# Two layers of graph attention on one core: where the second pass of layer 0 makes its masks, and in what order it issues its loads

## The chip, the cores and the metric

The kernel runs on one core of one Trainium2 chip, in float32. The metric is device time in microseconds (us). A tile has 128 partitions. TensorE is called PE in profiles (PEld is its weight load), VectorE DVE, ScalarE ACT, GpSimd POOL and SyncE SP.

## The reference

There are 4096 nodes with 512 features. Only layer 0 matters for the change. In it:

```
h = relu(layernorm(x))
node_att = softmax(h @ node_w, axis=0)
e = (h @ edge_w) @ (h @ edge_w).T            # 4096 x 4096, symmetric
e = where(adj > 0, e, -9e15)
edge_att = softmax(e, axis=1)
x = x + (adj * node_att * edge_att) @ (h @ weight) + bias
```

Layer 1 normalizes again and runs an attention with 8 heads over the same adjacency. Its logits are sums of a source and a target term.

## The kernel before, in words

The program has four stages, one after the other.

The first normalizes x and computes `sup` = h @ weight, kept in SBUF, and h @ edge_w, transposed. The second, the first pass over the scores, computes the upper half of the symmetric matrix e on TensorE (L288), stores it in device memory as `e_d`, and finds each row's maximum under the mask.

The third stage is the second pass of layer 0 (L321 to L594), and the change is there. It goes through 8 blocks b of 512 columns and, inside each, 32 tiles m of 128 rows, 256 steps in all. A tile is the transposed piece of the attention: 128 source nodes by 512 target nodes. For each:

- `load` (L337) issues on SP the load of `a`, the tile of adj transposed (256 KB, L356, 11 buffers). For tiles above the diagonal (m // 4 < b) it also loads the scores `et` as they are stored (L353); this text calls them direct tiles. For the four tiles on the diagonal it loads pieces of rows into `eb` (L349). At m = 0 it issues on GpSimd's queue the load of the row maxima `mb` (L342).
- `squares` (L359) serves tiles below the diagonal, whose scores are only stored as their mirror image. Once per four tiles it issues on SP 16 DMAs of 64 KB each (L366) into one `eb` tile (four buffers), which permute blocks of 32 x 32 so that VectorE's transpose of 32 x 32 blocks can finish the work.
- `turn` (L370) makes the transposed scores in PSUM: VectorE's transpose (L378) for squares, TensorE transposes (L384) for pieces on the diagonal, nothing for direct tiles.
- `exps` (L390) makes the mask `mk` = -9e15 where adj is 0 (L392, a tensor_scalar on VectorE), subtracts the maxima (L396), adds the mask to give `d` (L397), all on VectorE, and issues exp on ScalarE (L399).
- `weigh` (L402) multiplies by adj on VectorE, which gives `at` (L405, three buffers), and adds exp to the running sum `racc` on GpSimd (L412 once per block, L415 after).
- `gather` (L418) multiplies `at` with `sup` on TensorE: 4 products, 8 matmul instructions in the profile, into four PSUM banks (L435). At m = 8 it issues four loads of 256 KB on SP (L425). At the last tile of a block the row sums (L432) come before the products, and ScalarE copies the result out (L440).

After `weigh`, `finish` (L445) scales one of the four row tiles of the block before, on VectorE (L454), and stores it from GpSimd's queue (L455), in steps 2 to 5 of a block; `tail` (L529) feeds the start of the next part. In steps 3 and 4 of the first block `maxima` of the last column block is done as well.

The order of instructions in each engine's queue is that in which these functions are called: the loop at L564 to L576, with a list of stages and how many tiles each is ahead. The order of one step on VectorE is therefore: transpose of tile s+3, mask, subtraction and addition of tile s+2, product of tile s+1, and then what `finish` adds. On SP it is: squares (at every fourth step) for tiles s+11 to s+14, then scores and `a` of tile s+8. Queues run in order; an instruction that waits for a buffer or for data holds those behind it on its engine.

The fourth stage is layer 1 (from L596 on). The end of the third stage already computes its linear part (L505).

Of the kernel before, what the change touches and what calls it, by code (L numbers as in the profile page):

```python
# [8 lines left out]
FP = mybir.dt.float32  # L9
AF = mybir.ActivationFunctionType  # L10
ALU = mybir.AluOpType
# [4 lines left out]
P = 128  # L16
NEG_BIG = -9000000000000000.0
# [11 lines left out]
def kernel(  # L29
# [15 lines left out]
    nc = tc.nc  # L45
# [6 lines left out]
    BL = 512  # L52
# [47 lines left out]
    with tc.tile_pool(name="w0", bufs=1) as wp, tc.tile_pool(name="a0", bufs=2) as ap_, tc.tile_pool(  # L100
        name="a0s", bufs=8
# [126 lines left out]
    def maxima(i, acc, psum, pool):  # L228

        mx = pool.tile([P, TB], FP, name="mx")  # L230
        nc.vector.tensor_reduce(mx, rm[:, i * TB:(i + 1) * TB, i:NB], AX.X, ALU.max)
        pc = psum.tile([P, TB, P], FP, name="pt")
        for j in range(TB):
            nc.tensor.transpose(pc[:, j, :], acc[:, j * P:(j + 1) * P], ident)
        cm = pool.tile([P, TB], FP, name="cm")
        nc.vector.tensor_reduce(cm, pc, AX.X, ALU.max)
        nc.vector.tensor_tensor(mx, mx, cm, ALU.max)
        yield
        pm = psum.tile([P, BL], FP, name="pt")
        nc.tensor.transpose(pm[:TB, 0:P], mx, ident)  # L240
        ms = pool.tile([TB, P], FP, name="ms")
        nc.vector.tensor_copy(ms, pm[:TB, 0:P])
        nc.gpsimd.dma_start(mx_d[i], ms)


    with tc.tile_pool(name="mx", bufs=1) as mxp, tc.tile_pool(name="b_a", bufs=6) as adjp, tc.tile_pool(
        name="b_e", bufs=4
    ) as esp, tc.tile_pool(name="b_m", bufs=2) as mkp, tc.tile_pool(name="b_s", bufs=2) as sp, tc.tile_pool(
        name="b_p", bufs=6, space=PSUM
# [3 lines left out]
        loaded, masks = {}, {}  # L253
# [67 lines left out]
    with tc.tile_pool(name="c_a", bufs=11) as adjp, tc.tile_pool(name="c_b", bufs=4) as ebp, tc.tile_pool(  # L321
        name="c_e", bufs=9
    ) as etp, tc.tile_pool(name="c_w", bufs=3) as wkp, tc.tile_pool(name="c_t", bufs=3) as atp, tc.tile_pool(
        name="c_m", bufs=2
    ) as mxp, tc.tile_pool(name="c_o", bufs=4) as iop, tc.tile_pool(name="c_s", bufs=2) as sp, tc.tile_pool(
        name="c_p", bufs=1, space=PSUM
    ) as p_o, tc.tile_pool(name="c_q", bufs=3, space=PSUM) as p_t, tc.tile_pool(
        name="c_r", bufs=1, space=PSUM
    ) as p_r, tc.manual_schedule():
        steps = [(b, m) for b in range(NB) for m in range(NT)]  # L330
        blk = {}
        src, pts, aj, ex, at = {}, {}, {}, {}, {}

        def rows_of(m):
            return slice(m * P, (m + 1) * P)
# [34 lines left out]
        def turn(b, m):  # L370
# [16 lines left out]
                parts.append((slice(n * P, BL), eb[:, i, :] if m // TB == b else eb))  # L387
            src[b, m] = parts

        def exps(b, m):  # L390
            mk = wkp.tile([P, BL], FP, name="mk")
            nc.vector.tensor_scalar(mk, aj[b, m], 0.0, NEG_BIG, ALU.is_le, ALU.mult)  # L392
            d = wkp.tile([P, BL], FP, name="d")
            pt = pts.pop((b, m))
            for cs, part in src.pop((b, m)):
                nc.vector.tensor_tensor(pt[:, cs], part[:, cs], blk[b][0][:, cs], ALU.subtract)  # L396
            nc.vector.tensor_tensor(d, pt, mk, ALU.add)  # L397
            e = wkp.tile([P, BL], FP, name="ex")
            nc.scalar.activation(e, d, AF.Exp)  # L399
            ex[b, m] = e  # L400
# [44 lines left out]
        def finish():  # L445

            t, acc, oc, rs, xt = left.pop(0)
            b, j = divmod(t, TB)
            if j == 0:
                sc = sp.tile([P, TB], FP, name="sc")  # L450
                nc.vector.reciprocal(sc, rs)
                nc.vector.tensor_tensor(sc, sc, na[:, b * TB:(b + 1) * TB], ALU.mult)
                scale[b] = sc
            nc.vector.scalar_tensor_tensor(oc, acc, scale[b][:, j:j + 1], xt, op0=ALU.mult, op1=ALU.add)  # L454
            nc.gpsimd.dma_start(x1[rows_of(t), :], oc)  # L455
# [71 lines left out]
        end = len(steps)  # L527

        def tail(s):  # L529

            if s == -6:
                w_fetch()
            if -6 <= s and s + 6 < NT:
                fetch(s + 6)
            if s == -2:
                stats(0)
                stats(1)
                norm(0)
                stats(2)
                norm(1)  # L540
            if s >= 0:
                if 0 < s:
                    values(s - 1)
                if s + 2 < NT:
                    norm(s + 2)
                if s + 3 < NT:
                    stats(s + 3)
                if s == 0:
                    turn_h(0)
                if s + 1 < NT:  # L550
                    turn_h(s + 1)
                linear(s)
                if s > 1:
                    logits(s - 2)
                if s == WT + 2:

                    pt = p_t.tile([P, BL], FP, name="pt")
                    for h in range(HG):
                        nc.tensor.transpose(pt[:WT, h * P:(h + 1) * P], s_n[:, h, 0:WT], ident)
                    st = sp.tile([WT, HG, P], FP, name="s_t", bufs=1)  # L560
                    nc.vector.tensor_copy(st.rearrange("t h p -> t (h p)"), pt[:WT, :])
                    nc.gpsimd.dma_start(s_d.rearrange("h t p -> t h p"), st)

        stages = ((squares, 11), (load, 8), (turn, 3), (exps, 2), (weigh, 1), (gather, 0))  # L564
        for s in range(-11, end):
            for f, ahead in stages:
                if 0 <= s + ahead < end:
                    f(*steps[s + ahead])
                if f is weigh:
                    if left and s % NT > 1:  # L570
                        finish()
                    tail(s - end)
                    if s == 3:
                        ending = maxima(NB - 1, acc_z, p_t, sp)
                    if s in (3, 4):
                        next(ending, None)  # L576
# [10 lines left out]
        pt = p_t.tile([P, BL], FP, name="pt")  # L587
# [50 lines left out]
    with tc.tile_pool(name="p", bufs=2) as prp, tc.tile_pool(name="rl", bufs=2) as rlp, tc.tile_pool(  # L638
        name="io1", bufs=3
    ) as iop, tc.tile_pool(name="s1", bufs=1) as sp, tc.tile_pool(name="za", bufs=1) as zp0, tc.tile_pool(name="e3", bufs=2) as e3p, tc.tile_pool(  # L640
        name="zb", bufs=1
    ) as zp1, tc.tile_pool(name="e", bufs=3) as ep, tc.tile_pool(name="ac", bufs=2) as acp, tc.tile_pool(
        name="os", bufs=1
    ) as osp, tc.tile_pool(name="u", bufs=1) as usp, tc.tile_pool(
        name="p_x", bufs=1, space=PSUM
    ) as p_x, tc.tile_pool(name="p_v", bufs=1, space=PSUM) as p_v, tc.tile_pool(
        name="p_t1", bufs=1, space=PSUM
# [4 lines left out]
        zs_, ra, ex, e3, rl, pr, acc, pv, late = {}, {}, {}, {}, {}, {}, {}, {}, {}  # L652
# [272 lines left out]
        load(0, 2)  # L925
        first_e = ra[0, 0]
        exps(0, 0)
        ra[0, 0] = first_e

# [28 lines left out]
        scale(0, 1)  # L958

        stages = ((load, 3), (logs, 5), (exps, 1), (weigh, 1), (factors, 2), (scale, 2), (gather, 0))  # L960
        for s in range(len(steps)):
            for f, ahead in stages:
# [45 lines left out]
```

## Time and profile before

| | us |
|---|---|
| median of 3 runs | 2991.66 (2991.22 to 2992.32) |
| the profiled execution: time | 2991.82 |
| the profiled execution: span, first to last instruction | 2990.0 |
| busy in the span: TensorE | 2942.8 (98%) |
| busy in the span: VectorE | 2607.1 (87%) |
| busy in the span: GpSimd | 1340.9 (45%) |
| second pass of layer 0: first product on TensorE | starts at 716.53 |
| second pass of layer 0: row sums of block 7 | start at 1622.10 |
| VectorE's masks of this pass (L392), 256 | 219.3 in all, 0.857 each |
| VectorE's products (L405), 256 | 193.5 in all, 0.756 each |
| GpSimd's running sums (L415), 240 | 323.5 in all, 1.348 each |
| SP's loads of squares (L366), median to landing | 2.9 |

A row of groups reads: line, engine, operation, output<-inputs, shape, number; then busy time in all, the mean in ns; then the engine's idle time ahead of these instructions, and what ended it. A row of the timeline reads: start, duration, engine, line, operation, names, number. A row of the table by stretches reads: the stretch, its length, the busy time of each engine with its number of instructions, the granted clock of TensorE (1.00 is full), the share of the DMA engines and GB/s.

### The profile page before, as it was taken

The numbers are of one execution on the slowest core, as the hardware profiler recorded it, in microseconds if no ns is written. First come the engines' busy times: TensorE is split into PE (matmuls) and PEld (weight loads), VectorE is DVE, ScalarE is ACT, GpSimd is POOL, SyncE is SP. The second block draws the span as 40 slices with busy tenths as digits, with TensorE's granted clock in tenths as the row PEclk, the third lists the DMA queues.
The fourth block names the chain that finished last, engine by engine and source line by source line (L and its number), as shares of the span: only waits on it lengthen the run. The fifth ranks groups of instructions, "written<-read, shape, count | busy, mean of one in ns | idle before, by whom it ended". The sixth has DMA issues, their size and how long they took to land.

```text
span 2990.0 us, 43039 instructions
## 1 busy us (share of the span) xinstructions
PE 2942.8 (98%) x15371; PEld 1155.0 (39%) x15371; DVE 2607.1 (87%) x3596; ACT 1325.5 (44%) x1852; POOL 1340.9 (45%) x1042
## 2 busy tenths in 40 slices
PE   8999999998999999999999989999999999999998
PEld 4444444444344444444444433323222322232222
DVE  5434777778999999998997789999999999999998
ACT  2111111111112122122122368888777777777776
POOL 3401111112333343443443657575757575757574
PEclk9999999999999999999999999999999999999999
DMA  4205666667875674664553239696969696979795
GB/s 155 95 7 185 224 219 223 227 217 181 195 169 153 156 184 149 173 190 144 177 179 110 62 113 226 199 247 198 249 201 242 204 243 208 237 209 237 213 228 156
DMA packets 454055, 552.01 MB, mean 185 GB/s; under 512 B 261624, under 2 KB 287256, under 8 KB 453840
## 3 DMA queue, kind: packets, MB, share of 16 engines
q1 hardware_dynamic: 400816, 387.81, 42.1%
q0 software_dynamic: 51008, 157.51, 22.8%
q10 hardware_dynamic: 2016, 3.93, 0.4%
q8 instruction: 121, 1.98, 0.3%
q14 instruction: 94, 0.77, 0.1%
HBM read 409.47 MB, written 59.97 MB: 157 GB/s over the span
## 4 chain that ended last, share of the span: by engine, by line
PE 76%; DVE 11%; DMA 4%; SPq 3%; issue 3%; ACT 2%; POOL 0%; DVEq 0%; ACTq 0%; POOLq 0%
PE pv L788 22%; PE po L435 18%; PE pe L288 15%; PE dn L793 7%; PE ps L159 4%; PE po L505 4%; PE pe L166 4%; DVE pr L756 4%; SPq L366 3%; DVE mk L392 2%; DMA acc<-pr 2%; DVE at L405 2%; DVE pt L396 1%; DVE pt L378 1%; DMA eb<-e_d 1%
## 5 line engine op out<-in xcount | busy, mean ns | idle before, releaser
L788 PE MATMUL pv<-pr,sup 128*32 128x512 f32 x8192 | 1009.5, 595 | 9.4 <-POOL d_m L953 5.4
L435 PE MATMUL po<-sup,at 128*128 128x512 f32 x2048 | 899.7, 596 | 8.8 <-DVE at L405 6.8
L765 POOL TENSOR_TENSOR acc<-acc,pr 128x1024 f32<-128x1024 f32 x232 | 558.2, 2406 | 316.2 <-DVE pr L756 315.8
L756 DVE SCALAR_TENSOR_TENSOR pr<-z,g_m,ex 128x1024 f32<-128x1024 f32 x512 | 630.6, 1271 | 6.0 <-ACT ex L714 5.8
L435 PEld LDWEIGHTS po<-sup,at 128*128 128x128 f32 x2048 | 383.2, 190 | 504.4 <-issue 435.6
L415 POOL TENSOR_TENSOR racc<-racc,ex 128x512 f32<-128x512 f32 x240 | 323.5, 1348 | 457.9 <-ACT ex L399 455.9
L788 PEld LDWEIGHTS pv<-pr,sup 128*32 128x32 f32 x8192 | 288.6, 110 | 592.3 <-issue 527.4
L399 ACT ACTIVATE ex<-d 128x512 f32<-128x512 f32 x256 | 160.8, 630 | 708.4 <-DVE d L397 699.8
L288 PE MATMUL pe<-he_t,he_t 128*128 128x512 f32 x896 | 386.4, 592 | 0.0
L714 ACT ACTIVATE ex<-e 128x1024 f32<-128x1024 f32 x256 | 263.1, 1028 | 225.1 <-DVE pr L756 224.7
L756 DVE SCALAR_TENSOR_TENSOR pr<-z,g_m,e 128x1024 f32<-128x1024 f32 x256 | 328.2, 1282 | 10.3 <-PE pv L788 5.4
L793 PE MATMUL dn<-pr,d_m 128*2 128x512 f32 x1984 | 335.1, 592 | 0.0
L724 ACT ACTIVATE e<-e,ld_m 128x1024 f32<-128x1024 f32 x256 | 291.0, 1137 | 11.0 <-DMA e<-in_adj_t_dram 10.9
L753 DVE SCALAR_TENSOR_TENSOR pr<-rl,ngd_m,ex 128x1024 f32<-128x1024 f32 x224 | 284.7, 1271 | 1.6 <-ACT ex L714 1.2
L742 ACT ACTIVATE rl<-z,ngd_m,d_m 128x1024 f32<-128x1024 f32 x224 | 275.1, 1228 | 0.0
L288 PEld LDWEIGHTS pe<-he_t,he_t 128*128 128x128 f32 x896 | 169.2, 190 | 210.1 <-issue 190.5
L291 ACT COPY es<-pe 128x512 f32<-128x512 f32 (+2 forms) x144 | 79.2, 550 | 377.1 <-PE pe L288 377.1
L292 POOL DMA_DIRECT2D e_d<-es x144 | 78.6, 546 | 364.6 <-ACT es L291 359.1
L392 DVE TENSOR_SCALAR mk<-a 128x512 f32<-128x512 f32 x256 | 219.3, 857 | 3.8 <-DMA a<-in_adj_t_dram 3.8
L405 DVE TENSOR_TENSOR at<-ex,a 128x512 f32<-128x512 f32 x256 | 193.5, 756 | 13.9 <-ACT ex L399 9.5
L397 DVE TENSOR_TENSOR d<-pt,mk 128x512 f32<-128x512 f32 x256 | 176.9, 691 | 8.9
L293 DVE CUSTOM_DVE_ANT_0 mk<-pe,mk 128x512 f32<-128x512 f32 (+2 forms) x144 | 92.9, 645 | 99.7 <-ACT es L291 99.7
(173 smaller groups left out, 2606.0 us busy)
## 6 DMA issues: line engine op xcount, KB each, us to landing
e<-in_adj_t_dram SPq DMA_DIRECT2D x256, 512.0 KB, 5.6
acc<-pr POOLq DMA_DIRECT2D x152, 512.0 KB, 5.9
a<-in_adj_t_dram SPq DMA_DIRECT2D x256, 256.0 KB, 3.2
ar<-in_adj_dram SPq DMA_DIRECT2D x120, 256.0 KB, 2.9
e_d<-es POOLq DMA_DIRECT2D x120, 256.0 KB, 3.1
eb<-e_d SPq DMA_DIRECT2D x456, 64.0 KB, 2.8
ac<-in_adj_t_dram SPq DMA_DIRECT2D x112, 256.0 KB, 3.5
et<-e_d SPq DMA_DIRECT2D x112, 256.0 KB, 3.3
```

The source lines that it names most:

```text
L288: nc.tensor.matmul(pe[:, :w], he_t[i][:, k, (t % TB) * P:(t % TB + 1) * P], he_t[j][:, k, BL - w:], start=(k == 0), stop=(k == KC - 1))
L392: nc.vector.tensor_scalar(mk, aj[b, m], 0.0, NEG_BIG, ALU.is_le, ALU.mult)
L415: nc.gpsimd.tensor_tensor(racc, racc, e, ALU.add)
L435: nc.tensor.matmul(po[j], w[:, j * P:(j + 1) * P], sup[:, m, :], start=(m == 0), stop=last)
L714: nc.scalar.activation(x_, ra.pop((i, m)), AF.Exp)
L724: nc.scalar.activation(x_, ra[i, m], AF.Exp, bias=ld_m[:, h // HG, m:m + 1])
L742: nc.scalar.activation(r, zs_[i, 0], AF.Relu, bias=ngd_m[:, h // HG, m:m + 1], scale=d_m[:, h, m:m + 1])
L753: nc.vector.scalar_tensor_tensor(w, rl.pop((i, m)), ngd_m[:, h // HG, m:m + 1], x_, op0=ALU.subtract, op1=ALU.mult)
L756: nc.vector.scalar_tensor_tensor(w, zs_[i, k], g_m[:, h + k, m:m + 1], e3.pop((i, m)) if k == 3 else x_, op0=ALU.max, op1=ALU.mult)
L765: nc.gpsimd.tensor_tensor(acc[i, 3], acc[i, 3], w, ALU.add)
L788: nc.tensor.matmul(v[c][q][r * D + c0:r * D + c0 + Q, :], va[:, m, g * HG + k, c0:c0 + Q], pr[i, m, k][:, q * BL:(q + 1) * BL], start=(m = ...
L793: nc.tensor.matmul(dn[r * Q:r * Q + w.shape[1], :], w, src[:, q * BL:(q + 1) * BL], **fl)
```

## The change

Two things change. The mask leaves `exps` and becomes a function of its own, `masks`. It runs three tiles ahead and stands behind `exps` and ahead of `weigh` in the list, so on VectorE the mask of tile s+3 lies between the addition for tile s+2 and the product of tile s+1. And in the list of stages `load` now comes ahead of `squares`, and squares go out nine tiles ahead and not eleven.

```
-        src, pts, aj, ex, at = {}, {}, {}, {}, {}
+        src, pts, aj, mks, ex, at = {}, {}, {}, {}, {}, {}
...
+        def masks(b, m):
+            mks[b, m] = wkp.tile([P, BL], FP, name="mk")
+            nc.vector.tensor_scalar(mks[b, m], aj[b, m], 0.0, NEG_BIG, ALU.is_le, ALU.mult)
+
         def exps(b, m):
-            mk = wkp.tile([P, BL], FP, name="mk")
-            nc.vector.tensor_scalar(mk, aj[b, m], 0.0, NEG_BIG, ALU.is_le, ALU.mult)
             d = wkp.tile([P, BL], FP, name="d")
             pt = pts.pop((b, m))
             for cs, part in src.pop((b, m)):
                 nc.vector.tensor_tensor(pt[:, cs], part[:, cs], blk[b][0][:, cs], ALU.subtract)
-            nc.vector.tensor_tensor(d, pt, mk, ALU.add)
+            nc.vector.tensor_tensor(d, pt, mks.pop((b, m)), ALU.add)
...
-        stages = ((squares, 11), (load, 8), (turn, 3), (exps, 2), (weigh, 1), (gather, 0))
-        for s in range(-11, end):
+        stages = ((load, 8), (squares, 9), (turn, 3), (exps, 2), (masks, 3), (weigh, 1), (gather, 0))
+        for s in range(-9, end):
```

## The prediction

> **What bounds the kernel now.** I read the page's first part, then its table of 40 slices, then the table by stretches for the second pass of layer 0, one row for each block of 512 columns, and last the timeline inside a block. TensorE is busy 98% of the span, so only gaps on TensorE can be gained, and only in the stage the change touches.
>
> ```profile
> PE 2942.8 (98%) x15371; PEld 1155.0 (39%) x15371; DVE 2607.1 (87%) x3596; ACT 1325.5 (44%) x1852; POOL 1340.9 (45%) x1042
> ...
> L435 PE MATMUL po<-sup,at 128*128 128x512 f32 x2048 | 899.7, 596 | 8.8 <-DVE at L405 6.8
> L392 DVE TENSOR_SCALAR mk<-a 128x512 f32<-128x512 f32 x256 | 219.3, 857 | 3.8 <-DMA a<-in_adj_t_dram 3.8
> ```
>
> The busy figure flatters TensorE, because modelled ends fill short gaps. Block lengths are better. In the table by stretches (columns: length, then busy time of PE, PEld, DVE, ACT, POOL; the cuts are at each block's first L432 matmul) the blocks should all be equal, and the first ones are not:
>
> ```profile
> 716.53:830.85 114.32, 113.59 (x254) 46.89 (x254) 113.11 (x161) 19.54 (x32) 41.84 (x41) 0.98 0.81 178
> 830.85:950.88 120.03, 117.70 (x271) 48.06 (x270) 118.75 (x163) 22.77 (x37) 42.84 (x36) 1.00 0.62 156
> 950.88:1064.39 113.51, 113.23 (x271) 49.47 (x270) 111.34 (x158) 22.29 (x37) 43.05 (x36) 1.00 0.64 162
> 1064.39:1176.41 112.02, 111.96 (x272) 49.84 (x271) 107.04 (x153) 21.92 (x36) 44.15 (x36) 1.00 0.64 167
> 1176.41:1287.83 111.42, 111.42 (x271) 50.05 (x270) 105.97 (x153) 23.03 (x37) 45.68 (x37) 1.00 0.63 171
> ```
>
> Blocks 4 to 7 take 111.42 to 111.43 us: TensorE's floor, 32 tiles of 8 matmuls, each tile 3.434 us (a matmul starts every 0.429 in the timeline), plus transposes and row sums. Blocks 1, 2 and 3 are 8.61, 2.09 and 0.60 above it. In blocks 0 and 1 VectorE is busy 99% of the time. It is the bound there, and the timeline shows why. Two steps of block 0, on squares (tiles below the diagonal), VectorE and GpSimd:
>
> ```profile
> 735.57 0.70 DVE L378 STREAM_TRANSPOSE pt<-eb 128x512 f32<-128x512 f32 x1
> 736.20 0.40 DVE L392 TENSOR_SCALAR mk<-a 128x512 f32<-128x512 f32 x1
> 736.53 0.67 DVE L396 TENSOR_TENSOR pt<-pt,mb 128x512 f32<-128x512 f32 x1
> ...
> 756.57 0.68 DVE L405 TENSOR_TENSOR at<-ex,a 128x512 f32<-128x512 f32 x1
> 757.16 0.72 DVE L378 STREAM_TRANSPOSE pt<-eb 128x512 f32<-128x512 f32 x1
> 757.51 1.27 POOL L415 TENSOR_TENSOR racc<-racc,ex 128x512 f32<-128x512 f32 x1 [2.48 <-ACT ex L399]
> 757.79 1.27 DVE L392 TENSOR_SCALAR mk<-a 128x512 f32<-128x512 f32 x1
> 758.98 0.68 DVE L396 TENSOR_TENSOR pt<-pt,mb 128x512 f32<-128x512 f32 x1
> 759.70 0.69 DVE L397 TENSOR_TENSOR d<-pt,mk 128x512 f32<-128x512 f32 x1
> 760.31 0.68 DVE L405 TENSOR_TENSOR at<-ex,a 128x512 f32<-128x512 f32 x1
> ```
>
> The same mask takes 0.40 us when GpSimd is idle and 1.27 when the running sum started 0.28 before it: it ends when the sum has ended (758.78) and 0.3 more. A step is 3.74 us (756.57 to 760.31), over TensorE's 3.434. The step 735.57 to 738.50, whose mask is short, takes 2.93. The chain of waits puts 2.7% of the span on SP's issues (L366), but VectorE's rows in block 0 show no idle after 714; I take that share as attribution.
>
> **What the Trainium skill says.** "SBUF — State Buffer", section "Who interferes with whom": VectorE and GpSimd share one port pair as an exclusive lock; a tensor_scalar in a two-port mode, or a VectorE operation with two SBUF inputs against a GpSimd operation that reads SBUF, blocks fully behind whichever started first. The trace agrees: 0.42 becomes 1.27. "VectorE: DVE Perf Modes", section "Mode 2×_2P": fp32 tensor_scalar from SBUF to SBUF gets the double rate, tensor_tensor doesn't. The mask's 0.42 beside the addition's 0.69, same shape, agrees. "TensorE: Matmul & The Clock Gate", Part 1: after idleness the array runs at half clock until some 3.4 us of work. Here the granted clock is 0.50 from 712 to 720.
>
> **The change, part by part.**
>
> *The mask's place.* No instruction is added or removed: 256 masks, now between d(m+2) and at(m+1), made for tile m+3. Call T the end of d. Exp starts at T+0.09 and takes 0.63 (756.74 after 756.65), the sum starts at T+0.86 (757.51). The mask starts before T+0, holds its place about 0.33, the product follows at T+0.25 and has been read by about T+0.85. So neither meets the sum; the transpose and the subtraction after it have one SBUF input each and ran beside the sum unhindered already. A square step is then the sum of start-to-start gaps: product 0.60, transpose 0.63, subtraction 0.72, addition 0.61, mask 0.33 = 2.89 us. The observed 2.93 supports it. That is under 3.434, so TensorE takes over as the bound; of 0.85 saved per step only 0.31 reaches the end, in steps where VectorE has no lead left.
>
> *Direct tiles* (above the diagonal, 112 of 256) read two SBUF tensors in the subtraction (et, mb). Now: product at 1556.47, mask, subtraction at 1557.42 blocked for 1.76, next product 1559.90: 3.43, and TensorE kept up. Afterwards the subtraction is ready at T+0.84 and the sum at T+0.86: a tie. If the sum goes first, T+0.86+1.28, then 0.57 of subtraction and 0.71 of addition: again 3.42. If the subtraction goes first, this step is 2.25 and the next about 3.85, a mean of 3.05. I price direct tiles at nothing; the cover is TensorE's 3.434 and the three at buffers, which let VectorE run up to 6 us ahead. A late step spends that lead, not TensorE's time.
>
> *Buffers and the added wait.* A mask needs its a one tile sooner. Behind it on VectorE waits the product, and behind that TensorE. Loads go out eight tiles ahead, so five are left: nothing, once SP is ahead. mk has three buffers, two are used.
>
> *SP's order.* Squares issue 16 DMAs per four tiles, about 10 us of SP time; they move behind a of three further tiles (3 x 0.48 = 1.4 us later), and those a about 10 us earlier. In mixed blocks et or diagonal loads also pass ahead, at 0.42 each. Squares are issued ten steps before their transposes even where a waits for its buffer. GpSimd's queue order is unchanged, as is ACT's.
>
> *Start of the pass.* SP's first a goes out at 700.05, the second behind sixteen squares at 710.73; VectorE waits 3.79 for it:
>
> ```profile
> 710.73 1.91 SPq L356 DMA_DIRECT2D a<-in_adj_t_dram  x4
> ...
> 713.92 0.43 DVE L392 TENSOR_SCALAR mk<-a 128x512 f32<-128x512 f32 x1 [3.79 <-DMA a<-in_adj_t_dram]
> ...
> 716.53 2.93 PE L435 MATMUL po<-sup,at 128*128 128x512 f32 x3 [5.44 <-DVE at L405]
> ```
>
> Four a now go first, landing by about 705. From the first addition (709.44, end 710.13): mask to 710.4, two subtractions 0.33+0.59, addition 0.61, mask 0.33, product 0.68: first matmul near 713.05, 3.5 us sooner. The first squares then issue at 702 to 712, landing by 714.5, and are needed near 716.
>
> *The sum.* Block 0's floor from its first matmul: 31 tiles x 3.434 = 106.45, maxima's transposes 0.55, and five matmuls at 0.855 instead of 0.429 under the halved clock, 2.0: 109.0. It took 114.32: 5.3 too much. The clock loss stays: TensorE is still idle near 711 to 713, when the clock falls. Start 3.5 + block 0 5.3 + block 1 8.6 + block 2 2.1 + block 3 0.6 = 20.1. In block 1 the steps that finish block 0's rows (about 4.5 us, sums and stores in between) use up lead but no more: six steps near 23 us against TensorE's 21.2. Later stages just start sooner. The profiled execution's 2991.82 (span 2990.0) less 20.1 is 2971.7; it lies 0.16 above the median 2991.66, so **2971.6**.
>
> **The rivals.**
>
> *Loads become the bound in blocks 0 and 1.* SP takes 12.7 us per group of four (700.66 to 776.78 for six groups), against TensorE's 13.74, and the DMA share is 0.81. For: SP issues without a pause until 788; two groups took 13.69 and 14.13. Against: the mean leaves 1 us per group. At 14.13 for all 13 groups of these blocks: 13 x 0.39 = 5 us back, **2977**.
>
> *The start gains nothing,* say because the diagonal's tiles or the early squares hold VectorE as a did: 3.5 back, **2975**. Here the reordering of loads does not do what it says.
>
> *A slower direct tile.* The product, waiting for its buffer, takes the port at T+0.80, just before the sum; the sum then runs T+1.35 to T+2.63, the subtraction behind it: step 3.91. On all 112 direct tiles: 112 x (3.91 - 3.434) = 53 us, **3025**. It decides from 20.1/112 = 0.18 over 3.434, a step of 3.61. Against: losing 0.48 of lead ends the wait for the buffer, so it should not repeat. Its mild form, 3.58 to 3.66, ends near no change.
>
> **How the numbers follow.** Forecast 0.68; loads 0.14; start 0.08; slower direct tiles 0.06; mild form 0.04. A measurement of this kernel tells about 0.2%, 6 us, from no change. Faster by more: 0.68+0.14+0.08 = 0.90; within: 0.04; slower: 0.06. The low end is the clock loss gone too and a start 1 us better: 2968.5. The high end takes in both faster rivals together with a few us more of loads: 2981. The unknown costs lie within: the tie at direct tiles, 0 to +6 us if some steps repeat; SP's margin, 0 to 5; the start's clock, -2 to 0.
>
> **What would show it.** Right: masks at 0.42 nearly everywhere; block 1 near 111.5; first L435 matmul near 713; square steps at 3.43 with VectorE waiting for TensorE at L405. Wrong: product or subtraction rows of 1.3 to 1.9 in square steps; VectorE idle on DMA in blocks 0 and 1; blocks 5 to 7 above 111.43, which would be the direct tiles.

## The result, and the profile after

| | us |
|---|---|
| changed kernel, median of 4 runs | 2970.8 (2970.24 to 2974.0) |
| kernel before, median of 4 runs on the same chip | 2991.44 (2989.87 to 2992.32) |
| ratio of times, changed to before | 0.9934, 95% interval 0.9917 to 0.9951 |
| forecast | 2971.6, range 2968.5 to 2981.0 |
| the profiled execution of the changed kernel: time | 2974.0 |
| its span | 2972.2 |

The change is 0.66% faster, 0.8 us from the forecast. A later measurement of the same kernel (e9 below) gave 2971.2.

The same rows of the page after the change: engines, then the groups of TensorE's products and of the masks. Line numbers move by two behind the new function (L435 is now L437, L405 L407, L396 L398, L397 L399, L399 L401, L415 L417, L440 L442); the mask is still L392.

```profile
PE 2930.7 (99%) x15371; PEld 1159.4 (39%) x15371; DVE 2522.1 (85%) x3596; ACT 1326.1 (45%) x1852; POOL 1376.0 (46%) x1042
...
L437 PE MATMUL po<-sup,at 128*128 128x512 f32 x2048 | 886.7, 594 | 2.2 <-DVE at L407 2.2
...
L392 DVE TENSOR_SCALAR mk<-a 128x512 f32<-128x512 f32 x256 | 136.5, 533 | 1.9 <-DMA a<-in_adj_t_dram 1.9
```

The numbers of instructions in the first row are unchanged. The masks cost 136.5 us and not 219.3: 82.8 of the 85.0 us that VectorE is less busy. Counted in the timelines, 126 of the 256 masks took over 1 us before and 26 do now; in the 112 steps on squares it was 108, and is 1. GpSimd is 35 us busier with as much work: the rows of its running sums (L417) come to 358.3 us and not 323.5, because these sums now do more of the waiting.

The table by stretches, block by block, cut again at each block's first row-sum matmul:

```profile
713.32:822.58 109.26, 109.26 (x253) 48.41 (x254) 97.93 (x165) 20.17 (x32) 48.70 (x42) 0.98 0.86 195
822.58:934.01 111.43, 111.43 (x272) 50.05 (x271) 96.82 (x161) 22.29 (x36) 49.99 (x36) 1.00 0.67 169
934.01:1045.43 111.42, 111.42 (x272) 50.05 (x270) 96.63 (x157) 22.28 (x36) 50.70 (x36) 1.00 0.68 168
1045.43:1156.85 111.42, 111.42 (x271) 50.05 (x270) 94.99 (x154) 22.29 (x36) 50.00 (x36) 1.00 0.64 169
1156.85:1268.27 111.42, 111.42 (x271) 50.05 (x270) 95.67 (x149) 22.29 (x36) 49.64 (x36) 1.00 0.60 169
```

Blocks 1 to 7 now all take 111.42 or 111.43, the floor that blocks 4 to 7 had before. VectorE is busy 90% of block 0 and 87% of block 1, where it was 99%. The bound has gone from VectorE to TensorE, and that is why 85 us off VectorE give 20 to the kernel.

The timeline of VectorE and GpSimd in block 0, in a step on squares in which VectorE waits for nothing:

```profile
722.50 0.68 DVE L407 TENSOR_TENSOR at<-ex,a 128x512 f32<-128x512 f32 x1
723.10 0.72 DVE L378 STREAM_TRANSPOSE pt<-eb 128x512 f32<-128x512 f32 x1
723.12 1.28 POOL L417 TENSOR_TENSOR racc<-racc,ex 128x512 f32<-128x512 f32 x1 [1.67 <-ACT ex L401]
723.73 0.67 DVE L398 TENSOR_TENSOR pt<-pt,mb 128x512 f32<-128x512 f32 x1
724.43 0.69 DVE L399 TENSOR_TENSOR d<-pt,mk 128x512 f32<-128x512 f32 x1
725.04 0.42 DVE L392 TENSOR_SCALAR mk<-a 128x512 f32<-128x512 f32 x1
725.37 0.68 DVE L407 TENSOR_TENSOR at<-ex,a 128x512 f32<-128x512 f32 x1
```

The step is 2.87 us (722.50 to 725.37), where it was 3.74. The sum runs from 723.12 to 724.40, beside the transpose and the subtraction, and neither is longer for it; the mask comes when the sum is over and takes 0.42.

Once VectorE is two tiles ahead it waits for a buffer ahead of the product, and the step has TensorE's length. The profile puts this wait down to ScalarE, but the exp that this product reads was done a step earlier. By the program, what is left to wait for is one of the three `at` buffers, which TensorE frees:

```profile
885.33 0.41 DVE L392 TENSOR_SCALAR mk<-a 128x512 f32<-128x512 f32 x1
886.21 0.69 DVE L407 TENSOR_TENSOR at<-ex,a 128x512 f32<-128x512 f32 x1 [0.47 <-ACT ex L401]
886.27 1.76 POOL L417 TENSOR_TENSOR racc<-racc,ex 128x512 f32<-128x512 f32 x1 [1.67 <-ACT ex L401]
...
889.64 0.69 DVE L407 TENSOR_TENSOR at<-ex,a 128x512 f32<-128x512 f32 x1 [0.47 <-ACT ex L401]
```

From 886.21 to 889.64 is 3.43, TensorE's time for a tile. The late product now takes the port 0.06 before the sum, and the sum's row shows 1.76 in place of 1.28: GpSimd waits about 0.5, and nothing waits for GpSimd.

The start of the pass:

```profile
700.38 1.95 SPq L356 DMA_DIRECT2D a<-in_adj_t_dram  x4
...
710.38 0.41 DVE L392 TENSOR_SCALAR mk<-a 128x512 f32<-128x512 f32 x1
...
713.32 8.88 PE L437 MATMUL po<-sup,at 128*128 128x512 f32 x15 [2.23 <-DVE at L407]
```

Four loads of a go out first, the second mask has no idle time ahead of it (it had 3.79), and the first product starts at 713.32 and not at 716.53.

### The profile page after: what moved, and what is told of

It is laid out like the page before. It is cut to its first block, busy times and chain, and to the rows that moved or that the text cites. A ratio compares the mean times of both kernels' runs of the same rounds, so it can differ in the third digit from the quotient of the medians.

```text
span 2972.2 us, 43109 instructions
## 1 busy us (share of the span) xinstructions
PE 2930.7 (99%) x15371; PEld 1159.4 (39%) x15371; DVE 2522.1 (85%) x3596; ACT 1326.1 (45%) x1852; POOL 1376.0 (46%) x1042
## 4 chain that ended last, share of the span: by engine, by line
PE 85%; DVE 6%; DMA 4%; ACT 2%; issue 2%; POOL 1%; SPq 0%; DVEq 0%; ACTq 0%; POOLq 0%
PE po L437 30%; PE pv L792 20%; PE pe L288 15%; PE dn L797 7%; DVE pr L760 5%; PE ps L159 4%; PE po L507 4%; PE pe L166 4%; DMA acc<-pr 2%; DMA e<-in_adj_t_dram 1%; DVE pr L757 1%; PE pt L847 1%; ACT e L728 1%; POOL acc L769 1%; ACT ex L718 0%
## 5 line engine op out<-in xcount | busy, mean ns | idle before, releaser
L437 PE MATMUL po<-sup,at 128*128 128x512 f32 x2048 | 886.7, 594 | 2.2 <-DVE at L407 2.2
L437 PEld LDWEIGHTS po<-sup,at 128*128 128x128 f32 x2048 | 387.4, 190 | 480.7 <-issue 446.1
L417 POOL TENSOR_TENSOR racc<-racc,ex 128x512 f32<-128x512 f32 x240 | 358.3, 1493 | 390.7 <-ACT ex L401 389.0
L401 ACT ACTIVATE ex<-d 128x512 f32<-128x512 f32 x256 | 160.5, 630 | 664.7 <-DVE d L399 648.1
L407 DVE TENSOR_TENSOR at<-ex,a 128x512 f32<-128x512 f32 x256 | 195.3, 763 | 80.0 <-ACT ex L401 51.2
L399 DVE TENSOR_TENSOR d<-pt,mk 128x512 f32<-128x512 f32 x256 | 176.9, 691 | 8.8
L392 DVE TENSOR_SCALAR mk<-a 128x512 f32<-128x512 f32 x256 | 136.5, 533 | 1.9 <-DMA a<-in_adj_t_dram 1.9
```

Source lines behind the costliest of these rows:

```text
L407: nc.vector.tensor_tensor(w, e, aj.pop((b, m)), ALU.mult)
L417: nc.gpsimd.tensor_tensor(racc, racc, e, ALU.add)
L437: nc.tensor.matmul(po[j], w[:, j * P:(j + 1) * P], sup[:, m, :], start=(m == 0), stop=last)
```

## The experiments

All were timed side by side with the kernel before. Two theories were to be told apart. **The port**: the mask is long because GpSimd's sum holds the port that both need, and its new place ends that. **Something else**: the loads' order, or the mask's distance, does it, or the mask's length there has a reason of its own.

### e1: the masks alone

```
-        stages = ((load, 8), (squares, 9), (turn, 3), (exps, 2), (masks, 3), (weigh, 1), (gather, 0))
-        for s in range(-9, end):
+        stages = ((squares, 11), (load, 8), (turn, 3), (exps, 2), (masks, 3), (weigh, 1), (gather, 0))
+        for s in range(-11, end):
```

> The masks at their new place, the loads in the old order (squares eleven ahead, ahead of adj's). If the gain is the port that mask and running sum share, blocks 1 to 7 take 111.42 each as with the whole change and only the start is lost: first product near 716.5, 3.2 us later, 2974. If the order of the loads did it, blocks 0 and 1 stay at 114 and 120 and the time near 2988.

Measured: 2975.45 (2974.9 to 2976.95), ratio 0.9945 (0.9932 to 0.9957). In its table by stretches, blocks 0 and 1:

```profile
716.64:825.49 108.85, 108.85 (x254) 48.28 (x255) 97.73 (x165) 20.15 (x32) 48.82 (x42) 0.98 0.88 191
825.49:936.91 111.42, 111.42 (x272) 50.05 (x270) 96.84 (x161) 22.27 (x36) 50.01 (x36) 1.00 0.70 173
```

The blocks are at the floor without the new order of loads; only the first product is late, at 716.64. These are the port theory's numbers.

### e2: the loads alone

```
-        stages = ((squares, 11), (load, 8), (turn, 3), (exps, 2), (weigh, 1), (gather, 0))
-        for s in range(-11, end):
+        stages = ((load, 8), (squares, 9), (turn, 3), (exps, 2), (weigh, 1), (gather, 0))
+        for s in range(-9, end):
```

> The loads in the new order, the masks where they were. If the gain is the port, only the start is gained: first product near 713.3, block 1 still near 120, time 2988. If loads were the bound in blocks 0 and 1, the time is near 2971 to 2975.

Measured: 2988.06 (2986.02 to 2990.64), ratio 0.9986 (0.998 to 0.9993).

```profile
713.79:826.84 113.05, 112.51 (x254) 47.38 (x254) 111.80 (x161) 19.54 (x32) 42.30 (x41) 0.98 0.81 179
826.84:946.93 120.09, 117.72 (x272) 48.07 (x271) 118.81 (x163) 22.77 (x37) 42.87 (x36) 1.00 0.63 162
```

The first product comes at 713.79, 2.7 sooner, block 0 is 1.3 shorter, and block 1 stays at 120. At the end of block 0 this kernel is 4.0 us ahead (826.84, where it was 830.85), and it gains nothing after that. So the loads are worth about 4 us, all of it by the end of block 0. Which of the two does it, the order or the nine tiles in place of eleven, was not tried apart. The two parts of the change add up: 16 to 17 and about 4 give the whole 20.

### e3: the masks early, in their old place

```
-        stages = ((load, 8), (squares, 9), (turn, 3), (exps, 2), (masks, 3), (weigh, 1), (gather, 0))
+        stages = ((load, 8), (squares, 9), (turn, 3), (masks, 3), (exps, 2), (weigh, 1), (gather, 0))
```

> The masks three tiles ahead, as in the change, but in the old place on VectorE, between the transpose and the subtraction; loads in the new order. If it is the place that counts, the masks take 1.27 us again in steps on squares and the time is that of the loads alone, 2988. If it is the distance (the mask ready a tile before its addition needs it), 2971.

Measured: 2990.02 (2988.0 to 2993.08), ratio 0.9994 (0.9986 to 1.0002). VectorE and GpSimd in block 0:

```profile
757.19 0.72 DVE L378 STREAM_TRANSPOSE pt<-eb 128x512 f32<-128x512 f32 x1
757.54 1.27 POOL L417 TENSOR_TENSOR racc<-racc,ex 128x512 f32<-128x512 f32 x1 [2.48 <-ACT ex L401]
757.82 1.27 DVE L392 TENSOR_SCALAR mk<-a 128x512 f32<-128x512 f32 x1
759.01 0.69 DVE L398 TENSOR_TENSOR pt<-pt,mb 128x512 f32<-128x512 f32 x1
```

A mask that nothing needs for another tile still takes 1.27 behind the sum, and block 1 takes 120.09, the same as in e2. The median lies 2 us above e2's, which the blocks do not explain; this stays open. It is the place on VectorE that counts. That the mask runs three tiles ahead is only what makes the place possible: between the addition and the product it is too late for its own tile.

### e4: the kernel before, without the running sums

```
-                nc.gpsimd.tensor_tensor(racc, ex.pop((b, 0)), e, ALU.add)
-            else:
-                racc = blk[b][1]
-                nc.gpsimd.tensor_tensor(racc, racc, e, ALU.add)
+                nc.gpsimd.memset(racc, 1.0)
+                ex.pop((b, 0))
```

> The kernel before, with GpSimd's running sums left out (each block's sums are set to 1, so the rows are not normalized). Masks stay in the old place. If the sum's hold on the port makes the mask long, all masks take 0.42, steps on squares 2.9 us, and the time is that of the masks alone, 2974. If the mask is long there for a reason of its own, 2991.

Measured: 2975.3 (2973.99 to 2977.37), ratio 0.9945 (0.9932 to 0.9959), the same as e1. Its group of masks, all at the old place:

```profile
L392 DVE TENSOR_SCALAR mk<-a 128x512 f32<-128x512 f32 x256 | 106.3, 415 | 5.6 <-DMA a<-in_adj_t_dram 5.6
```

The mean is 0.415 us, and block 1 is at the floor:

```profile
824.67:936.10 111.43, 111.43 (x272) 50.05 (x271) 92.40 (x161) 22.27 (x36) 3.71 (x6) 1.00 0.68 169
```

Taking away the other user of the port gives what moving the mask gives. That the sum makes the mask long is shown, from both sides.

### e5: two buffers for the products

```
-    ) as etp, tc.tile_pool(name="c_w", bufs=3) as wkp, tc.tile_pool(name="c_t", bufs=3) as atp, tc.tile_pool(
+    ) as etp, tc.tile_pool(name="c_w", bufs=3) as wkp, tc.tile_pool(name="c_t", bufs=2) as atp, tc.tile_pool(
```

> The whole change with two buffers for the products and not three, so that VectorE can be one tile ahead of TensorE and not two. If the lead is what pays for the slow steps at the start of a block (26 us for six steps against TensorE's 21), about 2 to 3 us are lost at the start of each of blocks 1 to 7, 15 to 20 in all: 2986 to 2991. If those steps cost nothing anyway, 2971.

Measured: 2973.99 (2973.09 to 2975.62), ratio 0.9937 (0.9924 to 0.9951). The expectation that the lead pays was wrong. Blocks 1 and 2 stay at 111.42 and 111.43, and the later ones lose 0.25 each:

```profile
823.47:934.89 111.42, 111.42 (x271) 50.05 (x270) 96.00 (x161) 22.41 (x36) 51.29 (x37) 1.00 0.69 170
1046.32:1157.99 111.67, 111.67 (x272) 49.97 (x271) 97.92 (x153) 22.40 (x36) 49.01 (x37) 1.00 0.66 169
```

Five such blocks make 1.25 us, not 15 to 20. What costs the 0.25 was not followed up. The timeline of the changed kernel at the start of block 1, ScalarE and VectorE, shows what the expectation had missed:

```profile
824.54 0.59 ACT L442 COPY oc<-po 128x512 f32<-128x512 f32 x1 [5.80 <-PE po L437]
...
827.59 1.15 ACT L401 ACTIVATE ex<-d 128x512 f32<-128x512 f32 x2
828.26 0.69 DVE L407 TENSOR_TENSOR at<-ex,a 128x512 f32<-128x512 f32 x1 [3.04 <-ACT ex L401]
```

ScalarE's copies of the block's result wait for TensorE, and the next two exps stand behind them. VectorE, far ahead, waits 3.04 us for these. So part of the six slow steps (26.4 us from 822.86 to 849.30) is not work but VectorE's lead, waited away. With a smaller lead there is less to wait for: the steps of the same six tiles with two buffers are 3.43, 3.43, 4.25, 3.71, 4.62 and 3.71, 23.2 in all.

### e6 and e10: a warm start; e9: the change again

```
+        def warm(n):
+            po = blk[0][2] = blk[0][2] or [p_o.tile([P, F], FP, name=f"po{j}") for j in range(TB)]
+            for j in range(n):
+                nc.tensor.matmul(po[j], sup[:, 0, 0:P], sup[:, 0, :], start=True, stop=True)
...
+                if f is turn and s in (-1, 0):
+                    warm(1 - s)
```

(The products of block 0 then go to the same four tiles and overwrite them.)

> The whole change, and three matmuls of no use on TensorE ahead of the pass's first product (their results are overwritten), in the idle time near 710 to 713. If the half clock costs 2 us there, block 0 falls from 109.3 to about 107 and the time to 2969. If TensorE is held by VectorE there anyway, block 0 stays at 109 and the time at 2971.

> The whole change again, on the same chip and in the same rounds as the kernel with the warm start, so that the two can be compared: 2971, block 0 109.3 us.

> The whole change with the three matmuls of no use ahead of the first product, beside the change alone: block 0 at 107.2 as in the first look, the time 2.1 below the change alone, 2969. If something later gives the 2 us back, the same time as the change alone.

Measured: e6 2972.15 (2970.98 to 2972.26), ratio 0.993; measured again, side by side, e9 2971.2 (2970.95 to 2972.94) and e10 2971.67 (2968.49 to 2972.8), ratios 0.9932 (0.9919 to 0.9944) and 0.993 (0.9916 to 0.9943). Block 0 of e9, then of e10:

```profile
711.90:820.56 108.66, 108.66 (x253) 48.33 (x254) 98.16 (x165) 20.15 (x32) 48.54 (x42) 0.99 0.88 195
```

```profile
714.51:822.00 107.49, 107.35 (x253) 47.63 (x254) 97.43 (x165) 20.16 (x32) 44.90 (x42) 1.00 0.88 196
```

The third number from the end of a row is the granted clock: 0.99 in e9, full in e10. The extra matmuls shorten block 0 by 1.2 here and by 2.1 between the first profile of the change (109.26) and e6 (107.20). The two gains differ because the loss does: in the clock's records the half clock lasts 6.8 us in the first profile of the change (710.9 to 717.7) and 3.4 us in e9 (711.7 to 715.1).

The whole time does not show the gain, and the 2969 of the expectations did not come. The traces show two reasons. The first product starts at 711.90 in e9 and at 714.51 in e10, for the first pass ended later, so e10 is behind at the end of block 0 in spite of its shorter block. And in both traces with the extra matmuls the clock falls to 0.50 once more, at the start of layer 1's linear part, which it does not do in e9 (e9, then e10, where these eight matmuls take 5.40 us and not 3.70):

```profile
1607.74 3.70 PE L507 MATMUL po<-eb,d 128*128 128x512 f32 x8 [1.86 <-ACT d L501]
```

```profile
1609.17 5.40 PE L513 MATMUL po<-eb,d 128*128 128x512 f32 x8 [1.85 <-ACT d L507]
```

The 1.7 us lost there are about as much as was gained. The traces of e2 and e5 have the same second fall without extra matmuls, so it is not shown that these cause it. The gain in block 0 is seen in the traces, and no version of this study is shown to beat the change.

### e7: the change without the running sums

The edit is that of e4, on the changed kernel.

> The whole change with GpSimd's running sums left out (each block's sums are set to 1, so the rows are not normalized). If what is left of the waits for the port (products, subtractions and masks of 1.3 to 1.8 us) only uses up VectorE's lead, the blocks stay at 111.42 and the time at 2971. If they still cost TensorE time, it falls by more than 2.

Measured: 2972.71 (2971.3 to 2973.86), ratio 0.9932 (0.992 to 0.9945). Block 1 and block 7 take 111.42 and 111.43 as with the sums. What is left of the waits for the port costs TensorE nothing.

### e8: squares late

```
-        stages = ((load, 8), (squares, 9), (turn, 3), (exps, 2), (masks, 3), (weigh, 1), (gather, 0))
+        stages = ((load, 8), (squares, 5), (turn, 3), (exps, 2), (masks, 3), (weigh, 1), (gather, 0))
```

> The whole change with squares five tiles ahead and not nine, two before their transposes. If SP has room to spare in blocks 1 to 7, only block 0 can suffer, where SP issues without a pause: 2971 to 2974. If the early issue of squares is needed, sixteen issues of some 10 us against 6.9 us of warning leave about 3 us or more of wait per group of four, 28 groups, to be paid from the lead first: 3000 or more.

Measured: 2971.23 (2970.38 to 2974.77), ratio 0.993 (0.9917 to 0.9942). Block 0 takes 109.16, block 1 111.42, and the later blocks stay at the floor. Squares issued two steps ahead of their transposes are early enough in blocks 0 and 1 too. The loads of squares had room to spare.

## Why the prediction was right, point by point

The forecast's sum, against the trace:

| term | forecast | measured |
|---|---|---|
| start, first product sooner | 3.5 | 3.21 (716.53 - 713.32) |
| block 0 | 5.3 | 5.06 (114.32 - 109.26) |
| block 1 | 8.6 | 8.60 |
| block 2 | 2.1 | 2.09 |
| block 3 | 0.6 | 0.60 |
| sum | 20.1 | 19.56 |
| from block 7's row sums to the end | 0 | -1.76 (1367.90, then 1369.66) |
| the profiled executions | 20.1 | 17.82 |
| the medians | | 20.6 |

The terms for the blocks hold to 0.3 us. That the median came within 0.8 us of the forecast is partly luck: the four executions spread over 3.8 us, and the profiled one gained 17.8. The start varies too. In the nine traces with the new order of loads the first product begins between 711.90 and 714.51 (mean 713.1), in the three with the old order between 715.75 and 716.64 (mean 716.3); the means differ by 3.2.

**What bounded the kernel.** Right: VectorE in blocks 0 and 1, through the mask's wait for the sum. e4 and e1 show it from two sides. The share of the chain that the profile gave to SP's issues was, as the prediction took it, attribution: e2 changes that order, and block 1 stays at 120, block 0 at 113.

**The mask's new place.** Right: a step on squares of 2.87 us against 2.89 forecast. Its sentence that neither mask nor product meets the sum holds only while VectorE is behind. When it is ahead, the product starts close to the sum and does meet it, and then GpSimd waits. The rows that the prediction named as a sign of being wrong, products or subtractions of 1.3 to 1.9 in steps on squares, came only twice in 112 such steps (1.75 at 718.56, 1.53 at 792.31). The prediction's "masks at 0.42 nearly everywhere" was too strong as well: the median is 0.416, the mean 0.533, and nearly all of the long ones are in direct tiles.

**Direct tiles.** The tie that the prediction described is there. The changed kernel in block 5, VectorE and GpSimd:

```profile
1302.15 0.68 DVE L407 TENSOR_TENSOR at<-ex,a 128x512 f32<-128x512 f32 x1
1302.75 0.69 DVE L398 TENSOR_TENSOR pt<-et,mb 128x512 f32<-128x512 f32 x1
1302.77 1.80 POOL L417 TENSOR_TENSOR racc<-racc,ex 128x512 f32<-128x512 f32 x1 [2.15 <-ACT ex L401]
...
1304.77 0.68 DVE L407 TENSOR_TENSOR at<-ex,a 128x512 f32<-128x512 f32 x1
1305.04 1.53 POOL L417 TENSOR_TENSOR racc<-racc,ex 128x512 f32<-128x512 f32 x1 [0.47 <-ACT ex L401]
1305.37 1.75 DVE L398 TENSOR_TENSOR pt<-et,mb 128x512 f32<-128x512 f32 x1
...
1308.10 0.69 DVE L407 TENSOR_TENSOR at<-ex,a 128x512 f32<-128x512 f32 x1
```

The subtraction goes 0.02 before the sum, the next one 0.33 behind it: steps of 2.62 and 3.33, a mean of 2.98, where the prediction had 2.25 and 3.85, a mean of 3.05. Both means are under TensorE's 3.434. The rival of a slower direct tile did not come: blocks 4 to 7 stay at the floor.

**The lead that pays for slow steps.** The conclusion was right, block 1 at the floor, but its size was not. The six steps take 26.4 us and not 23. With two buffers the same six take 23.2, so the 3 us more are waiting that the lead itself brings, behind ScalarE's copies, and the prediction had no term for that.

**The start and the clock.** Right within 0.3 us in this execution. The forecast let the loss of the half clock stay, and it does: 0.50 from 710.9 to 717.7 in the changed kernel, until 4.4 us after the first product (3.2 in e9), around the time of work that the prediction quoted. e6 puts the loss at 2.1, e10 at 1.2.

**Loads as the bound.** This rival had a chance of 0.14. The waits of masks for a are 1.9 us in all, and TensorE shows no gap for them in block 0 (109.26 busy of 109.26). e8 shows that squares needed no early issue. The prediction has squares issued ten steps before their transposes; by the list of stages it is six for the first tile of a group and nine for the last. e8's two steps suffice, so the slip did no harm.

**Later stages.** In the profiled execution they took 1.76 us more, with the same code. e9's run from row sums to the end takes 1368.88 (2969.4 - 1600.52). Over all twelve traces this part takes 1367.26 (e8) to 1370.61 (e2); kernels with the masks at the new place lie between 1367.26 and 1369.76, the others between 1367.67 and 1370.61. So the 1.76 are within the differences between executions.

## What to carry to other kernels

When one instruction of a kind takes three times as long as its neighbours of the same shape, look at what the other engine runs at that time: moving the instruction by one place can be worth as much as removing the other work. Put such an instruction where the other engine has nothing to run, here right behind the addition, while ScalarE still computes the exp whose result starts the sum. And price the gain by the lengths of equal blocks against their floor, not by the busy time saved: of 85 us, 16 to 17 counted, because after that another engine is the bound.

## What the runs showed of the hardware

Who comes first to the port decides, however narrowly. With 0.02 to 0.06 us between them the sum waited behind VectorE's instruction (1.80 and 1.76 for a sum of 1.28), with 0.28 the mask waited behind the sum (1.27 for a mask of 0.42). The row's duration in the trace contains the wait. The order can alternate from step to step, as at 1302.75 and 1305.37. The wait ends somewhat before the other's row does: the product's row at 886.21 ends at 886.90, and the sum behind it ends at 888.03, which less its usual 1.28 gives an estimated start of work at 886.75.

TensorE's granted clock fell to 0.50 after about 3 us with only a few short transposes (707.7 to 710.9 in the changed kernel). By the clock's records the half clock at the start of the pass then lasted 3.41 us in e9, 6.83 in the first profile of the change and 10.24 in the kernel before: once, twice and three times the same length. Six extra matmul instructions in that gap, 0.59 us each and of the products' shape, kept the clock at 1.00 in e6 and e10.
